# Last two layers of a four-layer image block on one Trainium2 core: an order written out by hand, with each batch given out beside the next one's norm and projections

## Chip, core and metric

The kernel runs on one core of a Trainium2 chip. The metric is the device time of one execution in microseconds. Several executions agree within some tenths of a per cent, so about 0.5% is what a comparison of this kernel can tell from no change.

The engines, as the profile names them: PE is TensorE (PEld its weight loads), DVE is VectorE, ACT is ScalarE, POOL is GpSimd, and SP is SyncE, which here issues most of the DMAs. A name such as L1285 is line 1285 of the kernel before, where the text is about the kernel before.

## What is computed

The reference takes an image `x` of 4 batches, 128 x 128 places and 128 channels, in float32, and adds four layers to it in turn. Each layer sees a group norm of `x` (32 groups of 4 channels).

```python
x = x + L0(gn(x))     # deformable 3x3 convolution, 4 groups, relu
x = x + L1(gn(x))     # a scan over rows: row = row + relu(conv1d(previous row)), 9 taps
x = x + L2(gn(x))     # inputs @ Wself + (sum over columns) @ Wm + (sum over rows) @ Wk
x = x + L3(gn(x))     # triangle product, below

# L3, per batch
xn    = layer_norm(x) * norm_g + norm_b
left  = (xn @ left_w  + left_b)  * sigmoid(xn @ lgate_w + lgate_b)
right = (xn @ right_w + right_b) * sigmoid(xn @ rgate_w + rgate_b)
gate  = sigmoid(xn @ ogate_w + ogate_b)
out   = einsum('bkjd,bkid->bijd', left, right)
out   = (layer_norm(out, onorm_g, onorm_b) * gate) @ to_out_w + to_out_b
```

The change is in L2 and L3 only. They hold the last 1740 us of the span, from about 3935 us on.

## The kernel before

The sizes in the code are P = 128 channels, B = 4 batches, S = 128 rows and columns, NQ = 4 quarters of DQ = 32 channels each, and JB = 8 rows per block. L0 (`deform_layer`) has an order written out by hand; L1 (`scan_layer`) and the last two layers have not. There the compiler's scheduler sets the order of the instructions on each engine, from what the code issues and from the buffers that come free.

`scan_layer` leaves the result of L1 in DRAM as `x2T` (channels first), and gives back the statistics of its group norm and the sums along rows and columns. `message_and_triangle` then does everything else. It loads its weights through ACT's queue (`square`, `column`, the projections' `raw`), works the norm's gain and bias into one matrix `wcat` of four quarters and the output gate, and then works by batch in three parts.

- `taken_in(b)` is L2 and the norm of L3. The group norm of L2 is worked into the matrix `ws` and two message terms `z`. Then for each of 16 blocks of 8 rows: a load `x2c` (L1274), the sum of the two message terms in `zc` on POOL (L1276), two matmuls (L1282), the add into the image `X`, which stays in SBUF (DVE, L1285), and statistics (L1290). `zc` and the later `sq` share one buffer ("in_work"). When `X` is full, eight stores of 1 MB put it into `x3T` (L1295), and the group norm of L3 is made (`gn_part`, L1296; the centring matrix `cs`, L1301). Then the layer norm, for each 16 rows: centring matmuls (L1316), squares and the centred image on ACT (L1322, L1325), means of the squares by matmuls with 32 columns (L1331), and a square root (L1337). The factors lie on the wrong axis, so they go to DRAM as `stdT`, come back over 128 partitions for the reciprocal, go out again, and come back broadcast as `rwide` (L1340 to L1350). DVE multiplies them into `X` (L1354), and POOL sets the first channel to one (L1356), which carries the biases.
- `multiplied(b)` makes, for each quarter of the channels, 16 blocks of projections (8 matmuls each, L1369), a sigmoid (L1374) and a product written into `T` (L1375), then 8 output gates (L1382, L1386) that go to DRAM as `gateT`, then 32 products of left and right (L1393), whose copy overwrites `left` in place (L1397). `T` has four quarters and a fifth part for `right`. `X` and `T` have one buffer each.
- `given_out(b)` goes over the rows by fours. The layer norm of the products needs statistics of columns of `T` (L1409 and the small operations to L1423, by 16 rows); `u` is the normed column (three of four on ACT, L1438, one on POOL, L1434); it is transposed (L1451), scaled to `y` (L1453), multiplied by the gate that was stored (L1446 loads it, L1454 multiplies on POOL), and the output matmuls (L1461) add to the transposed `x3` (L1448, L1457). ACT copies the result out of PSUM (L1462), and SP stores it (L1463).

What sets the order between the batches is the end of the function. The batch given out goes beside the taking in of the next, two of its steps to one group, and the projections stand alone:

```python
for _ in taken_in(0):
    pass
for b in range(B):
    T = multiplied(b)
    after = taken_in(b + 1) if b + 1 < B else iter(())
    for _ in given_out(b, T):
        next(after, None)
        next(after, None)
    for _ in after:
        pass
```

All functions that the change touches:

Of the kernel before, what the change touches and what calls it, by code (L numbers as in the profile page):

```python
# [19 lines left out]
P = 128  # L20
# [1134 lines left out]
def message_and_triangle(tc, c, x2T, counted, w2, w3, out, x3T, gateT, stdT):  # L1155

    nc = tc.nc  # L1160
    stats2, sum_w, sum_h = counted
    wself_T, wm_T, wk_T = w2
    (norm_g, norm_b, left_w, left_b, right_w, right_b, lgate_w, lgate_b, rgate_w, rgate_b,
     ogate_w, ogate_b, onorm_g, onorm_b, to_out_w, to_out_b) = w3
    JB = 8
    with ExitStack() as ctx:
        wp = ctx.enter_context(tc.tile_pool(name="l3w", bufs=1))

        def column(v, name):
            t = wp.tile([P, 1], F32, name=name)  # L1170
            nc.scalar.dma_start(t, v.rearrange("(p o) -> p o", o=1))
            return t

        def square(v, name):
            t = wp.tile([P, P], F32, name=name)
            nc.scalar.dma_start(t, v)
            return t

        wself = square(wself_T, "wself")
        wm = square(wm_T, "wm")  # L1180
        wk = square(wk_T, "wk")
        outw = square(to_out_w, "outw")
        gcol = column(norm_g, "gcol")
        bcol = column(norm_b, "bcol")
        ogcol = column(onorm_g, "ogcol")
        obcol = column(onorm_b, "obcol")
        outb = column(to_out_b, "outb")
# [6 lines left out]
        NP_ = NQ * 4 * DQ + P  # L1194
        wcat = wp.tile([P, NP_], F32, name="wcat")
        with tc.tile_pool(name="l3prep", bufs=1) as prep, tc.tile_pool(
            name="l3ps_w", bufs=2, space=PSUM
        ) as ps_w:
            raw = prep.tile([P, NP_], F32, name="wraw")
            braw = prep.tile([1, NP_], F32, name="braw")  # L1200
            blocks = raw[:, 0 : NQ * 4 * DQ].rearrange("p (q n e) -> p q n e", q=NQ, n=4)
            bblocks = braw[:, 0 : NQ * 4 * DQ].rearrange("p (q n e) -> p q n e", q=NQ, n=4)
            both = ((left_w, left_b), (right_w, right_b), (lgate_w, lgate_b), (rgate_w, rgate_b))
            for n, (wgt, bias) in enumerate(both):
                nc.scalar.dma_start(blocks[:, :, n, :], wgt.rearrange("p (q e) -> p q e", q=NQ))
                nc.sync.dma_start(
                    bblocks[:, :, n, :], bias.rearrange("(o q e) -> o q e", o=1, q=NQ)
                )
            nc.scalar.dma_start(raw[:, NQ * 4 * DQ :], ogate_w)
            nc.sync.dma_start(braw[:, NQ * 4 * DQ :], ogate_b.rearrange("(o n) -> o n", o=1))  # L1210
            bwide = prep.tile([P, P], F32, name="bwide")
            nc.vector.tensor_scalar(bwide, c.ones, bcol, None, ALU.mult)
            gained = prep.tile([P, NP_], F32, name="gained")
            nc.vector.tensor_scalar(gained, raw, gcol, None, ALU.mult)
            less = prep.tile([P, P], F32, name="less")
            nc.vector.tensor_copy(less, c.ident)
            nc.vector.tensor_scalar(less[0:1], less[0:1], -1.0, None, ALU.add)
            for n0 in range(0, NP_, 512):
                n1 = min(n0 + 512, NP_)
                pw = ps_w.tile([P, 512], F32, name="prep_ps")  # L1220
                nc.tensor.matmul(
                    pw[:, : n1 - n0], lhsT=less, rhs=gained[:, n0:n1], start=True, stop=True
                )
# [21 lines left out]

        xs = {}

        def taken_in(b):

            X = xs[b] = big.tile([P, S, S], F32, name="X")  # L1250

# [299 lines left out]
```

## Time and profile before

| What | Value |
|---|---|
| Median of 3 executions | 5698.81 us (5684.14 to 5704.44) |
| The profiled execution's own time | 5676.25 us |
| Its span, first to last instruction | 5674.5 us |
| Mean granted TensorE clock | 0.949 |
| Busy: PE, DVE, ACT, POOL | 5005.7, 3220.7, 2558.2, 1153.9 us |
| Moved by DMA | 710.66 MB, mean 125 GB/s |
| First matmul of the scan's transposes | 3085.26 us |
| Last matmuls of the scan start | 3935.45 us |
| First add into X | 3958.31 us |

All durations in the text come from the profiled execution. A stage's row (from a view of windows) has the busy time of each engine with the number of instructions, then the mean clock that TensorE was granted, the busy share of the 16 DMA engines and what they moved. A line of waits reads: the waiting engine, what it was about to do, `<-` what released it, the total of the waits in us, how many, and the longest. A line of a timeline reads: start, duration, engine, line, operation, output and input, and how many instructions are merged in it.

### The profile page before, as it was taken

The numbers are of one execution on the slowest core, as the hardware profiler recorded it, in microseconds if no ns is written. First come the engines' busy times: TensorE is split into PE (matmuls) and PEld (weight loads), VectorE is DVE, ScalarE is ACT, GpSimd is POOL, SyncE is SP. The second block draws the span as 40 slices with busy tenths as digits, with TensorE's granted clock in tenths as the row PEclk, the third lists the DMA queues.
The fourth block names the chain that finished last, engine by engine and source line by source line (L and its number), as shares of the span: only waits on it lengthen the run. The fifth ranks groups of instructions, "written<-read, shape, count | busy, mean of one in ns | idle before, by whom it ended". The sixth has DMA issues, their size and how long they took to land. (4 is left out here: it accounts for less than half of the span.)

```text
span 5674.5 us, 162404 instructions
## 1 busy us (share of the span) xinstructions
PE 5005.7 (88%) x68920; PEld 4294.2 (76%) x68920; DVE 3220.7 (57%) x8190; ACT 2558.2 (45%) x5247; POOL 1153.9 (20%) x1013
## 2 busy tenths in 40 slices
PE   2898999899999999999998999998796896897885
PEld 1787788788887888788997999997384584674775
DVE  4676666665666666555554666666547337346350
ACT  1554454544544545445442333332334644645544
POOL 4222221201222102221000111112203304204203
PEclk9999999999999999999998999999998998998997
DMA  5776565665666656555543222221515516516324
GB/s 151 156 168 151 125 145 132 153 139 109 140 139 138 146 104 147 131 129 126 88 92 82 83 84 81 75 83 64 170 43 204 178 55 209 160 53 232 126 73 147
DMA packets 1273816, 710.66 MB, mean 125 GB/s; under 512 B 845645, under 2 KB 1112174, under 8 KB 1263862
## 3 DMA queue, kind: packets, MB, share of 16 engines
q1 hardware_dynamic: 1243538, 658.56, 46.3%
q10 hardware_dynamic: 29540, 41.60, 2.1%
q8 instruction: 545, 8.93, 0.7%
q14 instruction: 193, 1.58, 0.1%
HBM read 417.28 MB, written 282.55 MB: 123 GB/s over the span
## 5 line engine op out<-in xcount | busy, mean ns | idle before, releaser
L606 PE MATMUL conv_ps<-ring,wdef 128*128 128x192 f32 (+2 forms) x7632 | 1296.4, 319 | 8.4 <-DVE x1c L576 6.2
L514 DVE TENSOR_TENSOR m<-t_ps,tent 128x390 f32<-128x390 f32 x1548 | 806.0, 556 | 781.7 <-ACT tent L512 778.1
L606 PEld LDWEIGHTS conv_ps<-ring,wdef 128*128 128x128 f32 x7632 | 1142.7, 195 | 127.7 <-issue 64.1
L512 ACT COPY tent<-t_ps 128x390 f32<-128x390 f32 x1560 | 690.6, 487 | 650.3 <-PE t_ps L498 639.3
L498 PE MATMUL t_ps<-parts_of,spread 57*64 57x99 bf16 (+1 forms) x12384 | 742.6, 275 | 168.6 <-DVE m L514 147.3
L523 PE MATMUL v_ps<-m,pixels 60*64 60x108 f32 (+1 forms) x22704 | 813.0, 264 | 17.6 <-DVE m L514 10.3
L498 PEld LDWEIGHTS <-spread 57*64 57x64 bf16 x12480 | 578.2, 125 | 313.5 <-issue 266.1
L523 PEld LDWEIGHTS v_ps<-m,pixels 60*64 60x64 f32 x22704 | 673.6, 137 | 68.5 <-DVE m L514 23.6
L549 ACT COPY ring<-v_ps 128x432 f32<-128x432 f32 x1032 | 505.0, 525 | 446.5 <-PE v_ps L523 445.8
L420 POOL TENSOR_TENSOR off<-off,koff 72x512 f32<-72x512 f32 x128 | 162.6, 1271 | 1764.2 <-DVE off L417 1764.2
L1369 PEld LDWEIGHTS pair_ps<-wcat,X 128*128 128x128 f32 x4096 | 479.4, 194 | 48.8 <-POOL X L1356 20.1
L1369 PE MATMUL pair_ps<-wcat,X 128*128 128x128 f32 x4096 | 501.8, 281 | 16.2 <-POOL X L1356 15.1
L1110 PEld LDWEIGHTS own_ps<-diff,wconv 128*128 128x128 f32 x4064 | 494.9, 191 | 13.2
L1375 DVE TENSOR_TENSOR T<-pair_ps,sig 128x512 f32<-128x512 f32 x256 | 266.8, 1043 | 412.2 <-ACT sig L1374 403.0
L1110 PE MATMUL own_ps<-diff,wconv 128*128 128x128 f32 x4064 | 495.7, 273 | 0.0
L506 PE MATMUL t_ps<-parts_of,spread 57*64 57x130 bf16 x9288 | 455.1, 225 | 0.0
L1150 POOL TENSOR_TENSOR sum_h<-sum_h,x2c 128x512 f32<-128x512 f32 x128 | 162.4, 1269 | 1139.9 <-DVE x2c L1136 680.9
L438 DVE SCALAR_TENSOR_TENSOR parts<-off,parts 72x512 bf16<-72x512 f32 x384 | 297.2, 774 | 153.2 <-ACT parts L430 147.5
L1461 PE MATMUL one_ps<-outw,y 128*128 128x128 f32 x1024 | 236.3, 337 | 140.1 <-POOL y L1454 140.0
L1068 ACT ACTIVATE rowT<-x1T_ps,t_x,s_x 128x128 f32<-128x128 f32 x512 | 207.7, 567 | 313.2 <-PE x1T_ps L1064 297.0
L1461 PEld LDWEIGHTS one_ps<-outw,y 128*128 128x128 f32 x1024 | 197.2, 241 | 185.1 <-POOL y L1454 182.0
L506 PEld LDWEIGHTS <-spread 57*64 57x64 bf16 x9312 | 319.1, 108 | 0.2
(183 smaller groups left out, 6771.5 us busy)
## 6 DMA issues: line engine op xcount, KB each, us to landing
pixels<-tab SPq DMA_DIRECT2D x688, 123.8 KB
parts_of<-off SPq DMA_DIRECT2D x1032, 55.7 KB
off<-parts SPq DMA_DIRECT2D x64, 891.0 KB
tab<-rows SPq DMA_DIRECT2D x384, 128.0 KB
xin<-in_x_dram SPq DMA_DIRECT2D x128, 256.0 KB
x<-x1c SPq DMA_DIRECT2D x32, 1024.0 KB
x1rows<-x SPq DMA_DIRECT2D x128, 256.0 KB
x2T<-x2c ACTq DMA_DIRECT2D x128, 256.0 KB
```

Source lines behind the costliest of these rows:

```text
L438: nc.vector.scalar_tensor_tensor(parts[:, NSPLIT + i, h : h + RO, 2 : S + 2], off, 0.0, part, ALU.is_gt, ALU.mult,)
L498: nc.tensor.matmul(tp[h : h + HALF, 0, 0:n].rearrange("p (r c) -> p r c", c=PADW)[:, :, i:PADW:RX], lhsT=spread[0:k, kx // 2, i, h : h + H ...
L506: nc.tensor.matmul(tp[h : h + HALF, 1, i * PADW : (i + 1) * PADW], lhsT=spread[HALF : HALF + k, kx // 2, first + i, h : h + HALF], rhs=src ...
L512: nc.scalar.copy(tent[:, 0:n], tp[:, 0, 0:n])
L514: nc.vector.tensor_tensor(m, *pair, ALU.mult)
L523: nc.tensor.matmul(to[p1 : p1 + HALF], lhsT=pix[p0 : p0 + LANES, xb, :], rhs=m[p0 : p0 + LANES, :, RX * xb : RX * xb + w], start=True, sto ...
L549: nc.scalar.copy(to, bodies[side])
L606: nc.tensor.matmul(pc[:, at : at + rows, x0:x1], lhsT=wdef[:, side, k, :], rhs=v[:, :, k if v.shape[2] == NK else kx, x0 + kx : x1 + kx], ...
L1110: nc.tensor.matmul(own[:, n], lhsT=wt[:, 2 * j + n, :], rhs=diffs[h][:, n, :, j : j + V], start=False, stop=(n == 1 and j == NJ - 1),)
L1369: nc.tensor.matmul(pj[:, j], lhsT=X[:, j0 + j, :], rhs=wcat[:, q * 4 * DQ : (q + 1) * 4 * DQ], start=True, stop=True,)
L1375: nc.vector.tensor_tensor(T[:, q : NQ + 1 : NQ - q, :, j0 : j0 + JB], pj[:, :, 0 : 2 * DQ].rearrange("p j (n d) -> p n d j", n=2), sig.rea ...
L1461: nc.tensor.matmul(po[:, j], lhsT=y[:, j], rhs=outw, start=False, stop=True)
```

## The change

The function is cut into three. `last_weights` makes `wcat` and the small weights, and is called ahead of the scan. `message_terms` makes `ws` and `z` of all four batches at once, right after the scan. `last_layers` holds the rest, and hands its instructions to five engines in the order in which the code issues them (`tc.manual_schedule`).

The parts are generators whose steps are interleaved by the loop at the end. Batches alternate between two layouts of `T`. In an even batch quarter q of `left` lies in part q of `T`, at all 128 rows. In an odd batch it lies across all four parts, at the 32 rows of quarter q (`left`, `whole`, `column` in the diff). When a batch is given out by rows, 32 rows free one stripe across the four parts, and the next batch's quarter fits into it; so the products of a batch can be given out while the next batch's quarters are written.

Other edits: `x2c`, `zc` and `sq` share four buffers, `std`, `rwide` and `sig` another four, `x3` has four and the gates three. The result of a group is copied into the buffer of its `x3`. The four variance matmuls of 16 rows stand in a row, after the centring of the next block. The round trip of the norm factors is spread over the steps that follow (`divided`), and its last part falls among the projections. The product of `left` and `right` with their sigmoids is two instructions of DVE in place of one. The output gates stand among the projections, one for two blocks. Each group's gate and x3 are loaded one or two groups ahead. The statistics and the normed columns go by groups of four rows. For the last batch, which is given out alone, DVE in place of POOL multiplies by the gate, and POOL norms two columns of four in place of one.

The diff, cut to its core (`last_weights`, `message_terms`, `scaled` and `scales` hold the operations of the old parts in a new place):

```diff
+def last_layers(tc, c, terms, w, x2T, out, x3T, gateT, stdT):
+        X = big.tile([P, S, S], F32, name="X")
+        T = big.tile([P, NQ + 1, DQ, S], F32, name="T")
...
+        def left(b, q, j0, n):
+            k, j = divmod(j0, QS)
+            return T[:, q, :, j0 : j0 + n] if b % 2 == 0 else T[:, k, :, q * QS + j :][:, :, 0:n]
+        def whole(b, q, d):
+            if b % 2 == 0:
+                return T[:, q, d].rearrange("p d (k m) -> p d k m", k=NQ)
+            return T[:, 0:NQ, d, q * QS : (q + 1) * QS].rearrange("p k d m -> p d k m")
+        def column(b, j):
+            k, m = divmod(j, QS)
+            if b % 2 == 0:
+                return T[:, 0:NQ, :, j]
+            return T[:, k].rearrange("p d (q m) -> p q d m", q=NQ)[:, :, :, m]
...
+        def messages(b):
+            def fetch(y0):
+                if y0 < S:
+                    x2c = four.tile([P, JB, S], F32, name="x2c", tag="wide")
+                    nc.sync.dma_start(x2c, x2T[b, :, y0 : y0 + JB, :])
+                    zc = four.tile([P, JB, S], F32, name="zc", tag="wide")
+                    nc.gpsimd.tensor_tensor(
...
+            fetch(0)
+            fetch(JB)
             yield
             for y0 in range(0, S, JB):
-                zc = one.tile([P, JB, S], F32, name="zc", tag="in_work")
...
+                fetch(y0 + 2 * JB)
                 yield
...
+        def scaled(b):
...
             for j0 in range(0, S, 16):
                 nc.sync.dma_start(x3T[b, :, j0 : j0 + 16, :], X[:, j0 : j0 + 16, :])
             yield
...
+        def divided(b, j0, pv):
+            std = four.tile([P, 512], F32, name="std", tag="half")
+            nc.scalar.activation(std, pv, AF.Sqrt, bias=c.eps)
+            yield
+            nc.sync.dma_start(stdT[b, 0, tokens].rearrange("(q e) -> q e", q=4), std[0:P:32])
+            yield
+            rs = two.tile([P, 2 * JB], F32, name="rstd")
+            nc.sync.dma_start(rs, stdT[b, 0, tokens].rearrange("(p e) -> p e", p=P))
+            yield
+            nc.vector.reciprocal(rs, rs)
+            yield
+            nc.sync.dma_start(stdT[b, 1, tokens].rearrange("(p e) -> p e", p=P), rs)
+            yield
...
+        def multiplied(b, q):
+            for j0 in range(0, S, JB):
...
+                for n, to in enumerate((left(b, q, j0, JB), T[:, NQ, :, j0 : j0 + JB])):
+                    e = slice(n * DQ, (n + 1) * DQ)
                     nc.vector.tensor_tensor(
+                        to, pj[:, :, e].rearrange("p j d -> p d j"),
+                        sig[:, :, e].rearrange("p j d -> p d j"), ALU.mult,
+                    )
...
+        def given_out(b):
+            alone = b + 1 == B
...
+            for k in range(-6, NS_ + 1):
+                if 0 <= k - 1:
+                    nc.sync.dma_start(out[b, :, 4 * k - 4 : 4 * k, :], outs.pop(k - 1))
+                if 0 <= k + 2 < NS_:
+                    x3 = x3s[k + 2] = four.tile([P, 4, S], F32, name="x3")
+                    nc.sync.dma_start(x3, x3T[b, :, 4 * k + 8 : 4 * k + 12, :])
+                if 0 <= k + 1 < NS_:
+                    u = us.pop(k + 1)
+                    pt = single((P, 4, P))
+                    for j in range(4):
+                        nc.tensor.transpose(pt[:, j], u[:, j], c.ident)
+                    y = ys[k + 1] = two.tile([P, 4, P], F32, name="y")
+                    nc.scalar.activation(y, pt, AF.Identity, bias=w.obcol, scale=w.ogcol)
+                    (nc.vector if alone else nc.gpsimd).tensor_tensor(
+                        y, y, gates.pop(k + 1), ALU.mult
+                    )
+                if 0 <= k < NS_:
+                    y, x3 = ys.pop(k), x3s.pop(k)
...
+                for i in counts.get(k, ()):
+                    statistics(i)
+                    if i + 1 in groups:
+                        scales(groups[i + 1], i + 1)
+                if 0 <= k + 2 < NS_:
+                    u = us[k + 2] = two.tile([P, 4, P], F32, name="u")
...
+                if 0 <= k < NS_:
+                    nc.scalar.copy(x3, po)
+                    outs[k] = x3
+                k += 3 if alone else 2
+                if 0 <= k < NS_:
+                    gates[k] = three.tile([P, 4, S], F32, name="gate")
+                    nc.sync.dma_start(gates[k], gateT[b, :, 4 * k : 4 * k + 4, :])
+                yield
...
+        order = {getattr(mybir.EngineType, e) for e in ("PE", "Activation", "DVE", "Pool", "SP")}
+        ctx.enter_context(tc.manual_schedule(engines=order))
...
+        for b in range(B):
+            n = 0
+            while step(msgs):
+                if n < 4 or n % 2:
+                    step(out_of)
+                n += 1
+            for _ in scaled(b):
+                step(out_of)
+            for n, _ in enumerate(normed_start := normed(b)):
+                if n in (6, 14):
+                    step(out_of)
+                if n == 23:
+                    break
+            msgs = iter(())
+            for q in range(NQ):
+                for n, _ in enumerate(multiplied(b, q)):
+                    step(normed_start)
+                    if q + 1 == NQ:
+                        if n < 6 and n % 2:
+                            step(out_of)
+                        if n == 15:
+                            if b + 1 < B:
+                                msgs = messages(b + 1)
+                                step(msgs)
+                        elif n > 16 and n % 2:
+                            step(msgs)
+                    elif n in (1, 3, 5, 7, 9, 11, 15, 20):
+                        step(out_of)
+            out_of = given_out(b)
+        while step(out_of):
+            pass
...
+    w = last_weights(tc, c, wp, w3)
+    with tc.tile_pool(name="l2", bufs=1) as l2:
...
         counted = scan_layer(tc, c, l2, x1, w_conv, norms, x2T)
+        terms = message_terms(tc, c, wp, l2, counted, w2, w.outb)
...
+    last_layers(tc, c, terms, w, x2T, out, x3T, gateT, stdT)
```

## The prediction

> **What bounds the kernel now.** I read the share of busy time first: TensorE (PE) is busy for 88% of the span, so only its gaps are to be had. The change lies in the last two layers, which begin at about 3935 us of the 5674.5 us span. I then cut that part into stages, and asked for the busy time of each engine. One batch goes from 4680 to 5087 us; the last row is the giving out of the last batch.
>
> ```profile
> core 0: us, PE busy (x) PEld busy (x) DVE busy (x) ACT busy (x) POOL busy (x), PEclk, DMA share, GB/s
> 4680.00:4702.00 22.00, 11.12 (x39) 7.85 (x39) 20.76 (x85) 10.25 (x22) 5.93 (x7) 0.61 0.12 35
> 4702.00:4771.00 69.00, 45.33 (x180) 26.69 (x179) 58.32 (x87) 21.69 (x40) 42.12 (x31) 0.92 0.63 212
> 4771.00:4911.00 140.00, 111.12 (x548) 70.60 (x549) 51.32 (x124) 100.99 (x153) 50.85 (x56) 0.89 0.71 229
> 4911.00:5087.00 176.00, 172.72 (x1300) 152.54 (x1298) 61.92 (x60) 75.32 (x130) 3.81 (x3) 1.00 0.19 66
> ...
> 5493.00:5674.00 181.00, 100.39 (x512) 88.41 (x512) 49.75 (x176) 92.50 (x169) 58.16 (x64) 0.72 0.44 135
> ```
>
> In order: start of the giving out (22 us), messages (69), norm (140), projections and products (176, TensorE full and all else idle). The norm is the stage with room: no engine fills it. The last row is nobody's: TensorE 100 of 181 us, at 0.72 of its clock. The waits of 4680 to 5087 us (total, times, longest) say why:
>
> ```profile
> DVE X L1354 <- DMA rwide<-stdT: 53.4, 21, 9.5
> PEld one_ps L1461 <- POOL y L1454: 48.1, 26, 5.1
> POOL y L1454 <- DMA gate<-gateT: 22.7, 8, 6.2
> POOL zc L1276 <- DVE X L1285: 17.1, 10, 2.6
> DVE X L1285 <- POOL zc L1276: 6.4, 9, 1.3
> ```
>
> The last two are a ring: `zc` has one buffer, so the sum of the message terms (1.9 us on Pool) and the add into X (1.9 us on DVE) take turns. The first is the round trip of the norm factors through DRAM; the second and third are a group of four rows given out whose gate arrives late. What SyncE (SP) issued (start, duration) shows how late:
>
> ```profile
> 4769.95 8.24 SPq L1295 DMA_DIRECT2D x3T<-X  x8
> 4782.08 0.34 SPq L1463 DMA_DIRECT2D out_dram<-gate  x1
> 4782.46 1.26 SPq L1446 DMA_DIRECT2D gate<-gateT  x1
> ```
>
> Eight stores of 1 MB go first; the chain of waits has the output store behind them landing only at 4782.08 + 10.85 = 4792.9, 23 us after the first store was issued.
>
> **What the Trainium skill says.** "SBUF — State Buffer", Who interferes with whom: a DVE instruction with at most one SBUF input, outside the two-port modes, does not contend with GpSimd. The add into X reads PSUM and one SBUF tile, so `zc` may run beside it; the trace never shows that pair side by side, but X takes 1911 ns with Pool 61% busy and 1903 ns over the whole run. "TensorE: Matmul & The Clock Gate", What's actually happening: after an idle window of about 3.4 us the clock halves; the trace agrees in kind (0.61, 0.72 where TensorE has gaps, 1.00 where it has none). The same page, Architectural detail: ACT and DVE are strict FIFO. So a late operand in a written order holds all behind it; the trace of before cannot show what that costs here, since its scheduler chose another order. "TensorEngine Tiling (Array Packing)", When to Use Tiling: a stationary operand 32 wide allows fourfold column tiling. Here two variance matmuls (L1331) occupy 0.98 us against 1.91 for two full ones (L1316); with four strips in a row I estimate 1.3 for four.
>
> **The change, part by part.** All prices at full clock from the groups and the timeline of 4400 to 4800 us.
>
> *Prices.* One quarter of projections: 29.4 (sixteen blocks of 1.84) + 6.9 gates + 7.2 products = 43.5 us of TensorE. One group given out: TensorE 0.45 + 4 x 0.33 = 1.8; ACT 3 x 0.60 + 0.78 + 0.585 = 3.2; DVE 4 x 0.28 = 1.1. One message step: TensorE 1.72, DVE 1.76 + 1.19 = 3.0. Sixteen rows of norm: ACT 4 x 1.12 + 0.69 = 5.2, TensorE 3.4 + 1.3 = 4.7.
>
> *A cycle of the three in the middle* (before (5493 - 4273) / 3 = 407 us). Four of its sixteen message steps now lie among the products of the last quarter. The other twelve run beside eight groups' steps, DVE-bound: 12 x 3.0 + 8 x 1.1 + 2.4 for two sets of factors = 48 (before 22 + 69 = 91; the batch's message terms are worked out once, ahead). Scaling: its own chain was 7 us (4770 to 4777). In the new order three groups' steps stand between, and this adds a wait: the gate of row group 4 is loaded behind the 8 MB store, the written order puts that group's output matmuls ahead of the first centring matmul, and everything on TensorE queues behind it. Gate at 23, product 1.3, matmuls 1.8: 26 us. Bound: 10 if the loads overtook the store, 35 if output stores add their 10.85. I take 26. Norm: 8 x 5.2 = 42, plus two groups, 47. Quarters 0 to 2 carry eight groups each, TensorE-bound: 3 x (43.5 + 8 x 1.8) = 174; ACT has 16 x 0.6 + 8 x 0.6 + 8 x 0.585 + 8 x 3.2 = 45 of each 58 us and DVE 16 x 1.1 + 9 = 27, so both are hidden; if ACT's order failed, its 45 would add up to 13 each. The two halves of T cost DVE an extra 0.1 per block, hidden under 1.84. Tail of the round trip in quarter 0: 5 us (three dependent DMAs; 25 before, from 4073 to 4134 against 36 of work). Quarter 3: 43.5 + 3 x 1.8 + 4 x 1.7 = 56. Sum 48 + 26 + 47 + 174 + 5 + 56 = 356. Gain 51 each, 153 in all.
>
> *First batch* (before 3958 to 4273 = 315). Messages 16 x 3.0 = 48 (before 62), scaling 8 with no groups to wait for, norm 43, four quarters 174, tail 5, four next message steps 7: 285. Gain 30.
>
> *Last batch given out alone* (before 181). The gate product moves to DVE (two SBUF inputs, priced as L1354, 0.69), Pool takes two of four rows, loads go two to three steps ahead. Per group: ACT 2 x 0.6 + 0.78 + 0.585 = 2.6; DVE 1.8; traffic 768 KB, at the 307 GB/s that 135 GB/s in a 0.44 share make, 2.5; the output store must land before the buffer four groups on is loaded. I take 3.0; bounds 2.6 and 4.5 (before about 5.4). 15 us to the first group, 31 x 3.0, 4 to end: 112. Gain 69; 25 to 80.
>
> *Weights before the scan.* SP gets five short loads and ACT eleven ahead of the scan's own, and four preparation matmuls stand in front of its first transposes (3085 us, when nothing else is ready): last weight issued about 3085, landed 2 later, about 5 of matmul at the cold clock: +8, bounds +3 to +10. After the scan the chain was slowed by these issues; it now does four batches at once: 17 us from 3942.7, against a first X at 3958.3: +1.5, bounds -5 to +5. The x2c and store queues are otherwise in the same order there.
>
> *Sum.* 8 + 1.5 - 30 - 153 - 69 = -242: 5676.25 - 242 = 5434 for the profiled run. Its time is 0.4% under the median shown (5698.81), so on the median 5457; I add 5 for table loads, two of which (1.28 each way) now fall between sigmoids. Forecast **5462 us**.
>
> **The rivals.** *Half the gain.* Small stalls everywhere: 128 groups each lose 1 us because gate, x3 and output store are only a step or two ahead and SP waits in order on landings. 5462 + 128 = 5590. For it: 23 us behind the x3T store; 48.1 us of output matmuls waiting for y. Against: a step in the quarters lasts 6.3 us, and landings at low traffic take 2 to 3.
>
> *Slower: the written order turns each late load into a TensorE stall.* Before, 96 of the groups filled gaps and could be late for nothing. Now 39 steps per batch stand in the one order of TensorE. Lost time per group decides: the gain of 237 is eaten at 1.9 us a group, and 2.1 makes it slower by 0.5%. With the gate landing as late as in the norm stage of before (6.2 us longest wait; 22.7 over 8 waits, 2.8 each) at every group: 128 x 2.8 = 358, so 5820. Against: those waits were in a stage that moved 229 GB/s; the quarters will move 8 MB in 58 us, 140 GB/s.
>
> *More gain.* The loads overtake the store (-16 x 3) and the alone stage is ACT-bound (-12): about 5400.
>
> *It doesn't do what it says.* The listing of the built instructions shows the groups between messages and blocks as written, so I give this nothing of its own.
>
> **How the numbers follow.** Forecast case, 5390 to 5530: 0.66. Half gain, 5530 to 5670: 0.17. More gain, under 5390: 0.07. Slower: 0.07, the strip about no change: 0.03. The range 5375 to 5625 cuts 0.05 off the case of more gain, the last third of half gain (0.05) and the two cases above it (0.10). What a measurement can tell from no change is about 0.5%, so under 5670 is faster: 0.90; 0.03 within; 0.07 slower.
>
> **What would show it.** Stages: messages about 48 us with DVE over 90%; then a TensorE gap of 10 us or more ahead of the first centring matmul, released by Pool's y and it by the gate's load; quarters of 58 us with TensorE full at clock 1.00; the last stage about 112 us. The ring of zc and X gone from the waits. Wrong: quarters over 65 us with TensorE waiting for ACT or y; X adds lengthened beside zc (the port); a last stage over 140; a scan that starts over 10 us later.

## The result, and the profile after

The changed kernel takes 5460.09 us (median of 4, 5457.84 to 5461.96), beside 5691.48 us for the kernel before in the same comparison (5677.96 to 5704.44): a ratio of 0.9594, 95% interval 0.9568 to 0.9619. Its profiled execution took 5459.8 us with a span of 5458.1 us. Lines below are those of the kernel after.

First the share of busy time, from the head of the page: TensorE is 118 us less busy than before (5005.7), the span 216 us shorter. The busy time went down in the last layers (1382.1 us before, 1259.6 after), where the mean granted clock rose from 0.91 to 0.95: in the last batch's stage the same 512 matmuls took 100.4 us at 0.72 before and take 77.5 us at 0.88 now.

```profile
PE 4887.5 (90%) x68890; PEld 4229.0 (77%) x68890; DVE 3237.4 (59%) x8389; ACT 2536.8 (46%) x5206; POOL 1137.0 (21%) x1013
```

The view of windows, over the stages that the prediction named. One cycle, 4271 to 4630 us: messages (52 us), scaling (30), norm (52), quarter 0 (62), quarters 1 and 2 (113). The last row is the last batch given out alone.

```profile
core 0: us, PE busy (x) PEld busy (x) DVE busy (x) ACT busy (x) POOL busy (x), PEclk, DMA share, GB/s
4271.00:4323.00 52.00, 31.64 (x88) 13.49 (x86) 50.78 (x74) 9.42 (x16) 28.58 (x19) 0.93 0.52 162
4323.00:4353.00 30.00, 10.40 (x54) 9.87 (x55) 10.35 (x39) 10.25 (x20) 4.99 (x6) 0.62 0.94 359
4353.00:4405.00 52.00, 47.13 (x163) 17.59 (x161) 21.34 (x50) 43.48 (x52) 13.46 (x15) 0.93 0.43 135
4405.00:4467.00 62.00, 57.91 (x469) 53.11 (x470) 35.98 (x86) 40.66 (x71) 21.96 (x23) 1.00 0.59 188
4467.00:4580.00 113.00, 113.00 (x924) 104.58 (x923) 45.88 (x104) 83.62 (x150) 29.95 (x32) 1.00 0.44 148
5350.00:5458.00 108.00, 77.50 (x512) 66.27 (x512) 64.68 (x175) 73.98 (x132) 34.30 (x62) 0.88 0.68 219
```

The messages are DVE's (50.8 of 52 us). Quarters 1 and 2 are TensorE's without a gap (113.0 of 113), with eight groups given out under each: where TensorE made projections and products alone in 44 us before, it now also gives out the batch before, in 57. The second row is the hole: DMA engines full (0.94), TensorE, DVE and ScalarE busy for a third of it and POOL for a sixth. The timeline shows why (start, duration, engine, line, what; in brackets the idle time before and its releaser):

```profile
4322.86 8.26 SPq L1375 DMA_DIRECT2D x3T<-X  x8
4333.89 1.22 SPq L1622 DMA_DIRECT2D gate<-gateT  x1
4348.39 1.26 POOL L1588 TENSOR_TENSOR y<-y,gate 128x512 f32<-128x512 f32 x1 [16.07 <-DMA gate<-gateT]
4350.24 0.47 PE L1585 MATMUL one_ps<-ident,u 128*128 128x128 f32 x1 [14.21 <-POOL u L1613]
4353.07 3.19 PE L1435 MATMUL pair_ps<-X,cs 128*128 128x512 f32 x6
```

A gate loaded behind eight stores of 1 MB comes 14 us later; POOL's multiply waits, POOL's next normed column `u` is queued behind it, TensorE's transposes wait for `u`, and the first centring matmul, which needs none of it, waits in TensorE's line. It starts 30 us after the first store.

For comparing kernels I read stage times from each trace: messages end at the first x3T store, scaling at the first centring matmul, norm at the first projection, each quarter at the end of its last product. The first layer's code is the same in all kernels but one, yet it ends anywhere from 3065 to 3088 us in their profiled executions. So the experiments are judged by the *last layers*, from the first add into X to the end, and the ratio to the kernel before is given beside. Stages whose code is the same still vary: the three cycles took 1071.5 us in after and 1076.4 and 1079.1 in e10_early and e11_alone_free, which leave them as they are. So a difference of 8 us in the last layers, from one trace each, is about as small as can be told from none.

| us | messages | scaling | norm | quarters 0, 1, 2, 3 | sum |
|---|---|---|---|---|---|
| before, first batch | 60.2 | 6.6 | 47.9 | 68.1, 43.9, 44.4, 43.9 | 315.0 |
| after, first batch | 48.8 | 6.1 | 52.9 | 51.3, 43.9, 43.9, 49.0 | 295.9 |
| before, second | 90.3 | 7.2 | 89.7 | 85.1, 44.4, 44.4, 43.9 | 405.0 |
| after, second | 52.1 | 30.2 | 51.9 | 61.8, 56.9, 56.9, 50.3 | 360.1 |

Before, the last batch alone took 182.5 us, and the last layers 1716.2; after, 115.9 and 1483.2.

### The profile page after: what moved, and what is told of

Its sections match the earlier page's. It is cut to its first block, busy times and chain, and to the rows that moved or that the text cites. A ratio compares the mean times of both kernels' runs of the same rounds, so it can differ in the third digit from the quotient of the medians.

```text
span 5458.1 us, 162832 instructions
## 1 busy us (share of the span) xinstructions
PE 4887.5 (90%) x68890; PEld 4229.0 (77%) x68890; DVE 3237.4 (59%) x8389; ACT 2536.8 (46%) x5206; POOL 1137.0 (21%) x1013
## 5 line engine op out<-in xcount | busy, mean ns | idle before, releaser
L523 PEld LDWEIGHTS v_ps<-m,pixels 60*64 60x64 f32 x22704 | 673.0, 137 | 69.8 <-DVE m L514 24.7
L1500 DVE TENSOR_TENSOR T<-pair_ps,sig 128x256 f32<-128x256 f32 x512 | 282.6, 594 | 390.8 <-ACT sig L1497 390.7
L1492 PE MATMUL pair_ps<-wcat,X 128*128 128x128 f32 x4096 | 481.5, 276 | 5.2 <-DVE T L1500 3.1
L1497 ACT ACTIVATE sig<-pair_ps 128x512 f32<-128x512 f32 x256 | 152.1, 598 | 253.5 <-DVE T L1500 104.6
L1099 PE MATMUL both_ps<-carry,wsum 128*128 128x128 f32 x2032 | 268.3, 273 | 1.1 <-DVE carry L1133 1.1
```

Source lines behind the costliest of these rows:

```text
L523: nc.tensor.matmul(to[p1 : p1 + HALF], lhsT=pix[p0 : p0 + LANES, xb, :], rhs=m[p0 : p0 + LANES, :, RX * xb : RX * xb + w], start=True, sto ...
L1099: nc.tensor.matmul(both, lhsT=wsum[:, j, :], rhs=old[h][:, 1, :, j : j + V], start=(j == 0), stop=(j == NJ - 1),)
L1492: nc.tensor.matmul(pj[:, j], lhsT=X[:, j0 + j, :], rhs=w.wcat[:, q * 4 * DQ : (q + 1) * 4 * DQ], start=True, stop=True,)
L1500: nc.vector.tensor_tensor(to, pj[:, :, e].rearrange("p j d -> p d j"), sig[:, :, e].rearrange("p j d -> p d j"), ALU.mult,)
```

## The experiments

### What the overlap is worth, and what sets it

**e9_apart**: each batch is given out alone, before the next is taken in.

```diff
-            alone = b + 1 == B
+            alone = True
...
-            out_of = given_out(b)
-        while step(out_of):
-            pass
+            for _ in given_out(b):
+                pass
```

> The buffers, T's quarters and the written order as after, but no batch is given out beside the next: each is given out alone, at the end of its last quarter, in the form in which after gives out the last one. Prices from after's trace: stage alone 115 instead of 82 + 14.2 a quarter that it adds beside: messages 37, scaling 6, norm 53, quarters 51 + 44 + 44 + 49 and 115 alone make 399 a cycle against 358. So the overlap is worth 3 x 41 = 123 of the 233 us: last layers 1605 (1590 to 1620). If the overlap is what the change gains, nearly all is lost: 1690 or more. If the two compete for TensorE so that it is worth little: under 1530.

Measured: 5569.7 us, ratio 0.9818 (0.9791 to 0.9845); last layers 1605.0, where 1605 was expected. A cycle takes 398 us, quarters 1 and 2 take 43.9 each. So the overlap itself is worth 122 of the 233 us. The other 111 are what this kernel without any overlap already gains on the kernel before, which did give out a batch beside the taking in of the next: the last batch's stage (68 us, 182.5 to 114.3), the first batch (18), and three cycles of 398 us against 406 (25).

**e7_nosched**: the same code, but its order is not binding.

```diff
-        ctx.enter_context(tc.manual_schedule(engines=order))
```

> The same code without the line that makes the written order of the last layers binding: the scheduler may order the same instructions by its own costs. T's freed quarters, the buffers and the interleaved program text stay. If the order is what gains (the overlap of a batch given out with the next one's norm and projections), most of the 233 us of the last layers (1716 to 1483) is lost: 1600 to 1720. If the layout is what gains (the blocks across the freed quarters remove the wait for T, and any order that finds the operands ready does well), it stays within 30 of 1483, or is better, since a scheduler may put other matmuls ahead of the 14 us stall: 1440 to 1515.

Measured: 5437.03 us, ratio 0.9583 (0.9567 to 0.9599); last layers 1473.8, 9 less than after, at the edge of what can be told. So the binding order is not what gains; the interleaved program text over buffers that allow it is enough, and the scheduler makes of it nearly the same. Stage by stage it trades. Its windows for the second batch's scaling, norm and quarter 0:

```profile
4323.00:4337.00 14.00, 7.89 (x52) 7.52 (x53) 13.62 (x54) 7.06 (x15) 4.78 (x6) 0.76 0.98 400
4337.00:4383.00 46.00, 46.00 (x166) 17.34 (x164) 28.89 (x98) 42.24 (x52) 10.22 (x10) 1.00 0.57 192
4383.00:4465.00 82.00, 66.81 (x472) 56.51 (x471) 36.05 (x66) 55.68 (x89) 29.14 (x30) 0.94 0.57 186
```

The DMA engines are just as full behind the store (0.98), but the scheduler puts centring matmuls ahead of the late gate: scaling 14.5 for 30, norm 45 for 52 with TensorE never idle. It pays in quarter 0, 83 us for 62 (first batch 78 for 51), and gains 14 in the lone stage. One cost is in the trace: ScalarE loads its tables, 1.28 us each, 38 times in the last layers, and 20 times in after. In the first batch's quarter 0 it does so seven times, going to and fro between square roots and sigmoids, and once in after. How much of quarter 0 that explains was not tested.

**e4b_ring**: `zc` has one buffer again.

```diff
-                    zc = four.tile([P, JB, S], F32, name="zc", tag="wide")
+                    zc = one.tile([P, JB, S], F32, name="zc")
```

(`x2c` and `sq` have three buffers together. With the four of after, e4_ring, the kernel did not fit: 32 KB per partition were wanted and 28.56 left.)

> zc has one buffer of its own again, as in the kernel before, so that Pool's sum (1.9 us) and DVE's add (1.9 us) take turns; x2c and sq have the three others. The rest as after. If the written order makes the messages DVE-bound (3.05 us a step, 4.2 with a group given out), the ring of 3.9 us shows only in steps without a group: the first batch's 12 by 0.8 and 4 in each later one: messages of the first batch 49 to 59, of the others 52 to 55, last layers 1483 + 10 + 3 x 3 = 1502 (1497 to 1507). If the change lives from the ring's removal, each of 64 steps pays 0.8: +51, 1530 or more. If the ring was never a bound: within 5 us of 1483.

Measured: 5492.51 us, ratio 0.967 (0.9652 to 0.9688); last layers 1525.3, +42, between the two cases that were expected (1502, and 1530 or more). The first batch's messages went from 48.8 to 60.3 us, as in the kernel before (60.2); those of later batches from 51 to 58.7 (55 at most expected), since a step with a group does not hide the whole of the ring. The messages are 34 of the 42 us; the other 8 are in the norm and quarter 0, where `sq` has a buffer less and where they are no more than the spread. So the ring's removal is worth 34 to 42 us.

### The hole in the scaling

**e1_moved**: the three groups' steps of the scaling go into the messages.

```diff
-                if n < 4 or n % 2:
+                if n < 10 or n == 11:
                     step(out_of)
...
             for _ in scaled(b):
-                step(out_of)
+                pass
```

> The three given-out steps that stand inside the scaling are put into the messages ahead of the 8 MB x3T store (11 of the 12 message steps now carry one). Theory (the PE stall of 14 us is the gate of row group 4 loaded behind the store, held by the written order): the stage from the last message to the first centring falls from 30 to about 12 us, the messages grow by 3 x 1.1 = 3 to 6 us of DVE, so a cycle of 358 falls by 12 to 14, three cycles by 36 to 42: 5420 us (5412 to 5430). Rival A (the loads only move the wait: x3, gate and x2c loads crowd the messages): messages grow by 12 or more, no change, 5452 to 5465. Rival B (the store's traffic itself holds the norm, whoever stands behind it): the stage stays over 22 us with ACT's write of X waiting for the store, 5440 to 5460.

Measured: 5438.03 us, ratio 0.9579 (0.9563 to 0.9595); last layers 1463.2, 20 less where 36 to 42 were expected. The scaling fell from 30 to 8.4 us, further than expected, so the stall is what the theory says. But the messages grew by 10 (62 us, DVE 56 of them busy), norm and quarter 0 by 4 together. Of 21.5 us a cycle, 7 remain: three groups cost more among the messages than beside a stall.

**e2_queue**: the 8 MB store is issued by ScalarE.

```diff
-                nc.sync.dma_start(x3T[b, :, j0 : j0 + 16, :], X[:, j0 : j0 + 16, :])
+                nc.scalar.dma_start(x3T[b, :, j0 : j0 + 16, :], X[:, j0 : j0 + 16, :])
```

> The 8 MB x3T store is issued from ScalarE's queue instead of SyncE's; order of all else unchanged. If the gate load is late because it stands behind the store in one queue, it lands 2 to 5 us after its issue and the PE stall of 14 us goes: three cycles by 10 to 14, 5418 to 5430. If it is late because 8 MB fill the DMA engines whatever the queue, the load still takes over 10 us, 5450 to 5465. If ScalarE's 8 us of issuing delays its own work (scale s, then y and u of the given-out group), the gain is cut to a third: 5440 to 5455.

Measured: 5446.89 us, ratio 0.9589 (0.9573 to 0.9605); last layers 1484.6, no change. The timeline and the window of e2_queue in the second batch's scaling:

```profile
4332.49 13.22 ACTq L1375 DMA_DIRECT2D x3T<-X  x5
4345.77 0.78 ACT L1587 ACTIVATE y<-one_ps,obcol,ogcol 128x512 f32<-128x512 f32 x1 [13.09 <-DMA x<-x3T]
...
4331.00:4346.00 15.00, 4.29 (x20) 4.24 (x20) 3.03 (x12) 1.91 (x5) 0.00 (x0) 0.61 0.98 397
```

Now ScalarE is held: the last five stores take 13.2 us to issue, and its own `y` stands behind them. (The trace puts that idle time down to a landing; but `y` starts 0.06 us after the last issue ends, at 4345.71.) Scaling is 23 us instead of 30, with 5 more in messages that end later. `y` came later than the gate, so the stage does not tell when the gate landed; the DMA queues do. SyncE issued an output store, an x3 load and the gate's load, each of 256 KB, from 4332.70 to 4334.37 us. From 4344 to 4348 us its queue (q1) was still moving the last 0.22 MB of them, beside ScalarE's stores (q10):

```profile
q10 hardware_dynamic: 194, 1.45, 85.7%
q1 hardware_dynamic: 124, 0.22, 14.3%
```

From 4348 to 4352 us q1 moved nothing (0.00 MB). So the gate, issued last, landed 10 to 14 us after its issue here too, as the second case has it: the 8 MB fill the DMA engines (0.98, 397 GB/s) from either queue. The Trainium skill says as much ("DMA: Bandwidth & Descriptors", Issuing engines are not separate DMA queues: transfers of all engines run on the same DMA engines and interleave). Its sentence that another issuing engine saves only sequencer time, which is "usually small relative to the DMA itself", does not show the price of this edit: the 13.2 us of issuing are time in which ScalarE's own work waited.

**e5_spread**: two stores in the scaling, the other six among the norm's steps.

```diff
-            for j0 in range(0, S, 16):
+            for j0 in (0, 16):
...
             def centred(j1):
+                j = j1 + 32
+                if j1 % 16 == 0 and j < S:
+                    nc.sync.dma_start(x3T[b, :, j : j + 16, :], X[:, j : j + 16, :])
```

> The given-out steps stay in the scaling, but only 2 MB of the x3T store are issued there; the other 6 MB follow in pieces of 1 MB, each two pairs of centrings ahead of the rows that it reads being overwritten. If the stall is the 8 MB at about 400 GB/s (21 us, what the trace of after shows from 4323 us on) that stand ahead of the gate, 2 MB cost about 5 us: the scaling falls from 30 to 14 us, and the other 6 MB, 15 us of transfers, hide in the 52 us of the norm; three cycles by 13 to 16, last layers 40 to 48 us shorter than after's 1483 (1435 to 1443). Rival: the pieces stand ahead of the round trip of the norm's factors on the same queue, and TensorE waits for ScalarE's write of X behind a store: the norm grows by 8 to 15 in every batch, the first too (53 to 61 or more), last layers 1475 to 1500.

Measured: 5441.14 us, ratio 0.9587 (0.9571 to 0.9603); last layers 1471.6, 12 less. Both theories were half right: the scaling fell to 14.5 us as expected, so the delay goes with the bytes ahead of the gate; and the norm grew by 6 (58.8 in the first batch, which had no stall to lose and got 4.5 us slower), quarter 0 by 3. The norm is sensitive to what stands ahead of its small transfers, which leads to the next question.

### Why the norm takes 53 us and not 43

**e3_std**: `std` leaves the four buffers that it shares with `rwide` and `sig`.

```diff
-            std = four.tile([P, 512], F32, name="std", tag="half")
+            d0 = j0 // (4 * JB // 2) * 4
+            std = T[:, NQ, d0 : d0 + 4, :].rearrange("p d i -> p (d i)")
```

> The tile std (square root of the variances of 16 rows) leaves the four buffers that it shares with rwide and sig and lies in the free right-hand quarter of T, a place of its own for each 16 rows. Theory (the norm is 53 us and not 43 to 47 because ScalarE's square root waits for a buffer still held by rwide, whose load and multiply are late, and TensorE waits behind it): the norm falls by 6 to 10 us in each of four batches, 5458 - 32 = 5428 (5418 to 5436). Rival (ScalarE is simply full in the norm: 16 rows cost 6.6 us of it and not 5.2): no change, 5452 to 5465. Second rival: the norm ends earlier but quarter 0 waits for the round trip of the factors by as much: 5445 to 5460.

Measured: 5449.58 us, ratio 0.9596 (0.958 to 0.9612); last layers 1474.9, 8 less. In the first batch the norm falls from 52.9 to 40.7 us and quarter 0 rises from 51.3 to 62.6: the second rival. My theory of the buffer was right on where the wait was and wrong on what it was worth.

**e6_sigwide**: as e3_std, and `sig` leaves the four buffers too.

```diff
-                sig = four.tile([P, JB, 2 * DQ], F32, name="sig", tag="half")
+                sig = four.tile([P, JB, 4 * DQ], F32, name="sig", tag="wide")[:, :, 0 : 2 * DQ]
```

> std in the free right-hand quarter of T as in e3_std, and sig too leaves the four half buffers (it takes the wide ones, which the messages and the norm use), so that rwide alone has them. e3_std left the first batch's norm plus quarter 0 at 103 us (40.7 + 62.6 against 52.9 + 51.3), TensorE waiting 9.9 us for T, T for sig, sig for a half buffer held by a rwide whose row had not come. Theory (the shared ring is the miss of norm and quarter 0): the first batch's norm plus quarter 0 falls from 104 to 92 (88 to 95), those beside a batch given out from 114 to about 108; last layers 1483 - 12 - 3 x 6 = 1453 (1445 to 1465). Rival (the round trip of the last rows' factors takes that long whoever holds which buffer): the first batch stays at 100 to 104, last layers 1472 to 1484.

Measured: 5440.28 us, ratio 0.9587 (0.9571 to 0.9603); last layers 1475.1. Norm and quarter 0 of the first batch are 100.8 us together; the rival again. The timeline of e6_sigwide in the first quarter 0 shows a fixed beat:

```profile
4063.74 1.31 DVE L1425 TENSOR_TENSOR X<-X,rwide 128x512 f32<-128x512 f32 x2 [3.08 <-DMA rwide<-stdT]
4064.97 0.24 DVE L1410 RECIPROCAL rstd<-rstd 128x16 f32<-128x16 f32 x1
4065.24 0.32 SPq L1412 DMA_DIRECT2D stdT<-rstd  x1
4066.71 0.80 SPq L1418 DMA_DIRECT2D rwide<-stdT  x2
...
4070.15 1.30 DVE L1425 TENSOR_TENSOR X<-X,rwide 128x512 f32<-128x512 f32 x2 [3.08 <-DMA rwide<-stdT]
4071.36 0.25 DVE L1410 RECIPROCAL rstd<-rstd 128x16 f32<-128x16 f32 x1
...
4074.72 3.75 PE L1493 MATMUL pair_ps<-wcat,X 128*128 128x128 f32 x16 [8.03 <-POOL X L1426]
```

DVE waits 3.1 us for the broadcast row; the reciprocal of the next strip of 16 rows stands behind that multiply in the written order, the store of that reciprocal behind it on SyncE's queue, and the next broadcast load behind that store. One strip takes 6.4 us (4063.74 to 4070.15), though the norm before it, with ScalarE's part of eight strips, took only 40.9 / 8 = 5.1 a strip.

**e8_newest**: as e6_sigwide, and the strips under way are stepped newest first.

```diff
-                for d in list(dividing):
+                for d in dividing[::-1]:
```

> As e6_sigwide (std in T, sig in the wide buffers), and the strips of the norm that are between their steps are stepped newest first instead of oldest first: a strip's reciprocal and the issue of its transfers come ahead of the older strip's multiply, on which DVE waits 3.1 us for the broadcast row. Theory (the norm runs at the pace of the factors' round trip, 6.4 us for 16 rows, because DVE waits for a row with the next strip's reciprocal queued behind it and SyncE's next transfers behind that): the first batch's norm plus quarter 0 falls from 101 to 86 to 94, those beside a batch given out by 5 or more from 110; last layers from 1475 to 1430 to 1455. Rival (the pace is that of the transfers themselves, 8 MB of broadcast rows and 8 MB of x3T, or of ScalarE): within 4 us for each batch, last layers 1468 to 1480.

Measured: 5441.95 us, ratio 0.9588 (0.9567 to 0.9609); last layers 1464.5. Norm and quarter 0 of the first batch: 93.9 us for 100.8, just inside what the theory said (86 to 94). DVE's waits for broadcast rows in these two stages fall from 18.0 to 8.3 us. But the multiplies of a strip still follow those of the strip before by 5.5 to 6.4 us in five cases of seven, so the order is part of the beat and not all of it; what sets the rest, the transfers or another wait, was not tested. The three later batches did not move (110.8 on average, 110.6 in e6_sigwide), so the expected 1430 to 1455 was missed. So the written order costs the first batch 7 us; beside a batch given out something else holds the norm, and these runs don't name it.

### The lone stage and the weights

**e11_alone_free**: the binding order ends before the last batch is given out.

```diff
-        ctx.enter_context(tc.manual_schedule(engines=order))
+        written = ctx.enter_context(ExitStack())
+        written.enter_context(tc.manual_schedule(engines=order))
...
+        written.close()
         while step(out_of):
             pass
```

> The binding order ends before the last batch is given out; only that stage may be ordered by the scheduler. In e7_nosched it took 101.8 us against 115.9. Theory (in the written order the alone stage waits in line for the four sets of factors and for Pool's u, which a scheduler avoids): 100 to 106 us, last layers 1470. Rival (e7_nosched's gain came from statistics of finished quarters taken ahead, inside the last quarter of products, which the binding order up to there still forbids): 112 to 117 us, no change.

Measured: 5447.18 us, ratio 0.9593 (0.9572 to 0.9613); the lone stage took 101.1 us for 115.9, as the theory has it. The last layers took 1475.3, only 8 less, because the cycles, whose code is unchanged, came out 8 longer. In after most groups follow each other by 2.4 us, but 5.3 to 8.9 us pass at each new set of factors. Here ScalarE stands for 4.9 us until DVE has the sums for the next set:

```profile
5372.73 0.78 ACT L1587 ACTIVATE y<-one_ps,obcol,ogcol 128x512 f32<-128x512 f32 x1 [0.17 <-PE one_ps L1585]
5378.44 0.32 ACT L1568 ACTIVATE rs<-rs,eps 128x32 f32<-128x32 f32 x1 [4.93 <-DVE rs L1565]
5381.62 0.78 ACT L1587 ACTIVATE y<-one_ps,obcol,ogcol 128x512 f32<-128x512 f32 x1 [0.53 <-PE one_ps L1585]
```

The stage's waits, first in after, then in e11_alone_free (5346 to 5447 us):

```profile
POOL u L1613 <- DVE nm L1570: 89.2, 6, 50.4
PE one_ps L1585 <- ACT u L1615: 28.6, 24, 8.1
```

```profile
PE one_ps L1585 <- ACT u L1615: 8.7, 4, 6.8
DVE y L1588 <- DMA gate<-gateT: 19.2, 9, 2.7
```

POOL waited for each set of factors (`nm`) too. TensorE waited 24 times for ScalarE's normed columns, up to 8.1 us where a set was new; ordered freely, 4 times. What is late next is the gate.

**e10_early**: the weights are made ahead of the first layer.

```diff
+    wp = ctx.enter_context(tc.tile_pool(name="l3w", bufs=1))
+    w = last_weights(tc, c, wp, w3)
     norms, far = deform_layer(tc, c, small, x, w_off, b_off, w_def, x1, tabs, offs)
```

> The last layers' weights are loaded and combined ahead of the first layer instead of ahead of the scan. Theory (the 9.8 us by which the scan starts later against the end of the first layer are these loads and the 18 us wait for ogate_w, with nothing beside them): the scan's first matmul comes 8 to 11 us sooner after the first layer's last one (30.5 us in after, 20.7 before), and the first layer, bound by its own loads at its start, ends 0 to 4 us later: 5452 (5445 to 5458 beside after's 5460, the spread of the first layer apart). Rival: the loads delay the first layer's start by as much: no change in all, 5456 to 5465.

Measured: 5468.43 us, ratio 0.9624 (0.9601 to 0.9647). The scan followed the first layer by 18.6 us instead of 26.3, 7.7 sooner where 8 to 11 were expected. But the first layer ended at 3103.1 us, 15 above the latest of the twelve other profiled executions of changed kernels. The waits of its first 60 us:

```profile
PE wsum_ps L228 <- DMA woff<-in_w_off_dram: 12.2, 1, 12.2
PE prepb_ps L1213 <- DMA wraw<-in_rgate_w_dram: 10.3, 1, 10.3
```

In after the first of these lasts 3.9 us. The late start is carried to the layer's end: ScalarE's first `tent` (a copy of the first layer) starts at 123.1 us, where all other traces have 105 to 107, and at ten later points of the layer e10_early is behind the latest of them by 9 to 18 us. So in this execution the loads delay the first layer by more than they save ahead of the scan, the rival's side. It is the slowest of four (5457.23 to 5479.75 us), and the interval of the ratio overlaps with after's: the place gains nothing, and that it loses is not shown.

### Together

**e12_together**: the edits of e8_newest, e1_moved and e11_alone_free.

> e8_newest, e1_moved and e11_alone_free in one kernel. They act in different stages, so the stage times should add: e8_newest took the first batch from 296 to 286 and each later cycle by 3, e1_moved each cycle by 7, e11_alone_free the last stage from 116 to 101. Last layers 1483 - 10 - 3 x 3 - 3 x 7 - 15 = 1428 (1420 to 1440), and with after's 3975 ahead of them 5403, 0.949 to 0.953 of before. Rival (the groups moved into the messages put their gate and row loads among the norm's, so that the gains of the norm and of the scaling are the same microseconds): last layers 1445 to 1460.

Measured: 5401.48 us, ratio 0.9515 to the kernel before (0.9499 to 0.9532); last layers 1426.9, where 1428 was expected. First batch 287.2 us, cycles 347.4, 346.5 and 344.8, lone stage 101.0. The gains add, as they should if they lie in different stages. Intervals against the same kernel before do not overlap with after's (0.9568 to 0.9619).

## Why the prediction was right

It forecast 5462 us; the median is 5460.09. By the spans of the profiled executions, its sum was -242 us, and -216.4 was measured:

| Term of the sum, us | on record | measured |
|---|---|---|
| weights ahead of the scan | +8 | +9.9 (16.4 to 26.3 between first layer and scan) |
| the scan and the terms after it | +1.5 | -1.5 (the scan 847.6 to 845.2, then to the first add into X 20.9 to 21.8) |
| first batch | -30 | -19.1 |
| three cycles | -153 | -147.3 |
| last batch alone | -69 | -66.6 |
| first layer | 0 | +8.2 |
| sum | -242 | -216.4 |

The last line before the sum is not shown to be an effect of the change: that layer's end lies at 3081.5 us here and at 3073.3 in the execution before, within the 23 us over which it varies. So the sum promised 26 us too much, 8 in the first layer and 18 in the terms. That 5460 comes so near 5462 is luck: the forecast stood 28 us above its sum, 23 because the median before lay above the profiled execution and 5 for table loads, and the kernel after has no such distance (profiled 5459.8, median 5460.09). By these medians the gain was 231.4, against the 237 that the forecast left; by four later sets of executions of the kernel before (medians 5672 to 5678) it would be 212 to 218. The terms are the better measure.

Point by point:

- *Messages 48*: 51.3 on average, DVE-bound as said. Thirteen adds into X fall into the stage (24.7 us of DVE from 4271 to 4323 us), not twelve: the last step put among the products is added after them. The ring's price was right for the first batch (e4b_ring).
- *Scaling 26*: 29.8. Place, mechanism and chain were as written, with one more link: it is `u`, queued on POOL behind the waiting `y`, that TensorE waits for. e1_moved, e2_queue and e5_spread show that bytes ahead of the gate set it. The bound of 10 needs fewer bytes in front: e5_spread had 14.5.
- *Norm 43, 47 beside two groups*: 52.9 and 51.7. This is the step that failed. "8 x 5.2" priced ScalarE's work alone. e6_sigwide shows that ScalarE can run so (40.9 us), but then quarter 0 pays; the pace is that of the factors' round trip, 6.4 us a strip, in an order that puts each reciprocal behind a waiting multiply. "Tail 5" saw only the end of it. It cost the first batch 12.7 us (52.9 + 51.3 against 43 + 43.5 + 5), all of the 10.9 that the first batch's term lacks. Of these, the buffers and the order of e8_newest give back 10.3, 6.9 by the order. Beside a batch given out, norm and quarter 0 took 113.7 us for 47 + 58 + 5, and neither edit brought that under 110.6 on average.
- *Quarters 0 to 2 with the tail 179*: 175.8. Eight groups cost 13.0 us a quarter (56.9 - 43.9), where 14.4 was on record.
- *Quarter 3, 56*: 50.3, and 45.2 in the last batch, which has no messages to start. It was given the matmuls of three groups (5.4 us) and four message steps (7). But 37 of a batch's 39 steps are done by then, and the two that are left have the output matmuls of one group (45.2 - 43.9 = 1.3); and three message steps come before the last product (5.1). So a cycle of 356 was met by 357 with its errors cancelling: 3 + 4 + 5 over, 3 + 7 under.
- *Lone stage 112*: 115.9. Its price of 3.0 a group, put between two bounds, was right as an average (3.2) and not as a pace: 2.4 for most groups, under the lower bound of 2.6, and a stop of 5.3 to 8.9 at each of the four later sets of factors. e11_alone_free shows that 15 us of it are the order's.
- *Four table loads more*: 20 of 1.28 us for 16 in the last layers, as counted.

"Half the gain" and "slower" fell because the late loads stay in one place: quarters 1 and 2 have TensorE full. "More gain" was for the most part a matter of order: e12_together, which also moves two buffers, puts no group's load behind the store and shortens the lone stage, and so comes to the 5400 that this rival named.

Still open: what holds the norm beside a group at 49 to 52 us, what keeps the strips of the first batch at some 6 us in e8_newest, and what the freed quarters are worth by themselves. No kernel here has the overlap without them, so the 122 us of the overlap are theirs and the interleaving's together.

## What to carry to other kernels

Price a stage by the slowest loop through it, round trips to DRAM included, and not only by its busiest engine: a buffer freed in front of such a loop moved 12 us from one stage to the next and gained 1. In a written order, ask of each instruction that can wait what stands behind it that does not need to: here a gate held centring matmuls, and a multiply held the next strip's reciprocal. Write by hand the interleaving that a scheduler would not find, and then try leaving it free: here the whole came out the same within the spread, better where a load or a set of factors was late, worse in quarter 0.

## What was not expected of the hardware

The prediction's first skill place held for the big pair: the add into X takes 1896 ns where `zc` runs beside it (1903 before, where the two took turns). But a DVE instruction with both inputs in SBUF can be held up by one of POOL's, as the timeline of after shows:

```profile
4292.38 1.89 POOL L1332 TENSOR_TENSOR zc<-z 128x1024 f32<-128x1024 f32 x1 [2.33 <-PE pair_ps L1345]
...
4292.72 1.60 DVE L1562 TENSOR_TENSOR both<-st 128x32 f32<-128x32 f32 x1
4294.24 0.17 DVE L1563 TENSOR_TENSOR apart<-st 128x16 f32<-128x16 f32 x1
```

The 23 instructions `both` that meet POOL idle take 0.19 us; here it ends with POOL's `zc` (4294.32 and 4294.27). In the kernel before, one beside a gate product takes 1.28 us (at 4390.26). Not every one is held: at 4742.84 us in after, a `both` takes 0.18 us while a gate product is under way on POOL. The Trainium skill has this case ("SBUF — State Buffer", Who interferes with whom: two SBUF inputs contend with a POOL instruction that reads SBUF), and the trace agrees but for that one. The prediction had read only the half that it needed: in the lone stage DVE's gate product, which has two such inputs and was priced 0.69, took 0.97 us in the 23 of 32 cases beside POOL's `u`, and 0.69 in the others.

Four variance matmuls on four column strips take 1.06 us, where 1.3 was estimated from two in 0.98. And to issue eight stores of 1 MB holds ScalarE for 8.3 us in the first batch of e2_queue, where nothing goes on beside them, as long as SyncE in after (8.2); in the later batches, beside SyncE's transfers, it took 13 to 15 us (15.1 from 4330.65 to 4345.72).
